# Adding the residual in layer 1 by an accumulating DMA in a two-layer graph kernel

## The chip, the cores and the metric

The kernel runs on one core of a Trainium2 chip, in float32 throughout. The metric is the device time of one execution in microseconds, as the median over several runs; lower is better. The core has TensorE (PE in the profile; PEld is its loading of weights), VectorE (DVE), ScalarE (ACT), GpSimd (POOL) and SyncE (SP). Each has its own instruction queue and works it off in order. DMAs are issued from such a queue and carried out by 16 DMA engines.

## The reference

There are 16 batches of 1024 nodes with 512 features, one dense weighted adjacency matrix of 1024 x 1024, and two residual layers.

```python
# layer 0
h = relu(layernorm(x));  x = x + (adj @ h) @ W0 + bias
# layer 1
h = relu(layernorm(x)) @ W
s1, s2 = h @ a[:F], h @ a[F:]
e   = leaky_relu(s1[:, :, None] + s2[:, None, :], 0.2) * adj
att = softmax(e, axis=2)
x   = x + elu(att @ h + beta * h)
```

The last line is the one that the change concerns. With z for the argument of elu, elu(z) = relu(z) + min(exp(z), 1) - 1. So the output is x1 + elu(z) = relu(z) + min(exp(z), 1) + (x1 - 1), where x1 is what layer 0 gave. The constant -1 is already in the bias of layer 0, so that x1 - 1 is what layer 0 writes out.

## The kernel before, in words

Layer 0 runs over the 16 batches first. For each it leaves three things in DRAM: `x1d[b]` (x1 - 1, four blocks of 128 x 1024), `ud[b]` (the normalised rows) and the logits `s1d`, `s2d`.

Layer 1 then runs over the batches, each in two stages. `layer1_a` multiplies the unnormalised attention matrix with the rows u, by a seven-product scheme in place of eight block products: 14 steps of 8 matmuls with 512 columns. `layer1_b` multiplies the outcome with W in the same way: 14 steps of 4 matmuls with 256 columns. After each step k the function `after(k)` emits the small work planned for that place: first what `later[k]` holds, then what the plan of the batch holds. All instructions keep the order in which they are emitted on their engine, and SP's DMAs too. Steps over 13 of `layer1_b` are carried over to the next batch's `layer1_a`, so that step 14 there is step 0 here.

The plan of a batch prepares the softmax of the next one. `masked` lets ScalarE form leaky_relu(s1 + s2) and VectorE multiply it by a mask row block and take the maximum; there are 8 mask blocks of 512 KB per batch, loaded by SP into the two buffers of the pool `ld`. `spread_max` sends the maxima through DRAM (`md`, `mall`) to all partitions, `exp` takes exponentials, `turn` transposes them into `pT`, `spread_sum` does with the sums what `spread_max` did (`sd`, `sall`), and `diagonal` adds beta times the sum to the diagonal. `right_sum` (`pT_T`) and `u_sums` (`ul_S`) form the operands of the seven products; `load_u` fetches the rows. In `SOFTMAX_A` (lines 1147 and following) the mask blocks 2 to 7 are asked for at the steps 0 to 5 of `layer1_a`, and the blocks 0 and 1 at the steps 11 and 12 of the preceding `layer1_b`. In batches 1 to 8 a row block of the last batch is normalised on the side (`late`).

The output of `layer1_b` comes in eight parts, each 128 x 512: node half nh, feature half oh, and q. For each part `elu` (line 884) emits:

- `parts`: ScalarE computes r = relu(z) and ez = exp(z), in two pieces each. They go to a buffer of the pool `b4` (12 buffers, also used for e and for the products) and to one of `b2`.
- `total`: two or three steps later VectorE forms d = min(ez, 1) + d, where d is a half of the tile `x1`, and GpSimd adds r to it.
- `store`: seven steps after the part, SP writes the whole tile to the output by four DMAs of 128 KB, once for two feature halves. For the four tiles these lie at steps 3, 4, 5 and 6 of the next `layer1_a`.

The tile `x1` (128 x 1024, pool `xp` with 4 buffers) is filled by `load_x1`, one SP load of 512 KB for each of four tiles at the steps 7 to 10 of `layer1_a` (line 1231). In the last batch (`end`) VectorE does both sums, and ScalarE's queue issues some of the stores.

Of the kernel before, what the change touches and what calls it, by code (L numbers as in the profile page):

```python
# [29 lines left out]
F32 = mybir.dt.float32  # L30
AF = mybir.ActivationFunctionType
ALU = mybir.AluOpType
AX = mybir.AxisListType

P = 128
Q = 32
# [29 lines left out]
def kernel(  # L66
# [12 lines left out]
    B, N, D = x.shape  # L79
# [4 lines left out]
    HD = D // 2  # L84
# [4 lines left out]
    b4 = ctx.enter_context(tc.tile_pool(name="b4", bufs=12))  # L89
    up = ctx.enter_context(tc.tile_pool(name="up", bufs=7))  # L90
    ld = ctx.enter_context(tc.tile_pool(name="ld", bufs=2))
    xp = ctx.enter_context(tc.tile_pool(name="xp", bufs=4))
# [17 lines left out]
    class InOrder:  # L110
# [9 lines left out]
    pe, dve, act, pool, sp = (  # L120
        InOrder(e) for e in (nc.tensor, nc.vector, nc.scalar, nc.gpsimd, nc.sync)
    )

    def add(o, i0, i1, op=ALU.add):
        dve.tensor_tensor(o, i0, i1, op=op)
# [368 lines left out]
    def node_rows(t, b):  # L494

        return [t[b, ts(s, SN), :].rearrange("(g q) d -> q g d", q=Q) for s in range(G)]
# [49 lines left out]
    def beside(plan):  # L546
        def run(k):
            for f, *args in plan.get(k, ()):
                f(*args)

        return run
# [49 lines left out]
    x1d = {}  # L601
# [272 lines left out]
    x1s = {}  # L874
    later = {}

    def layer1_b(b, plan):

        rs = sms[b].rs
        rows = node_rows(out, b)  # L880
        end = b == B - 1
        zs = {}

        def elu(nh, oh, q, z, k):

            r = b4.tile([P, 2, HD], F32, tag="b4", name=f"r_{b}_{nh}{oh}{q}")
            g0 = HC * nh + 2 * q
            ez = zs.pop((nh, oh, q), None)
            if ez is None:
                ez = b2.tile([P, 2, HD], F32, tag="b2", name=f"ez_{b}_{nh}{oh}{q}")  # L890

            def parts():
                for i in range(2):
                    sc = rs[:, g0 + i : g0 + i + 1]
                    act.activation(r[:, i, :], z[:, i, :], AF.Relu, scale=sc)
                    act.activation(ez[:, i, :], z[:, i, :], AF.Exp, scale=sc)

            if end or ez is not z:
                parts()
            else:  # L900
                later.setdefault(k + 1, []).append(parts)
            x1 = x1s[b, nh, q]

            def total():
                d = x1[:, :, ts(oh, HD)]
                dve.scalar_tensor_tensor(d, ez, 1.0, d, op0=ALU.min, op1=ALU.add)
                (dve if end else pool).tensor_tensor(d, d, r, op=ALU.add)

            def store():
                for s in range(G):  # L910
                    (act if end and nh and s % 2 else sp).dma_start(
                        out=rows[s][:, ts(2 * nh + q, 2), :], in_=x1[ts(s, Q)]
                    )

            later.setdefault(k + (1 if end else 2 if ez is not z else 3), []).append(total)
            if nh != oh:
                later.setdefault(k + (1 if end else 7), []).append(store)

        products = NODES_LAST if end else P5_EARLY
        at = {p[0]: 2 * n for n, p in enumerate(products)}  # L920
        weighted1 = []

        def part(nh, oh, q, ps):
            zs[nh, oh, q] = b2.tile([P, 2, HD], F32, tag="b2", name=f"z_{b}_{nh}{oh}{q}")
            act.copy(zs[nh, oh, q], ps)

        def rest(nh, oh, q, ps, k):
            z = zs[nh, oh, q]
            add(z, ps, z)
            elu(nh, oh, q, z, k)  # L930

        def done(prod, q, ps):
            if prod == "p1":
                weighted1[0].fork("W", q, ps)
            elif prod == "p6":
                part(0, 1, q, ps)
            elif prod == "p5":
                part(1, 1, q, ps)
            elif prod == "p7":
                rest(1, 1, q, ps, at[prod] + q)  # L940
            elif prod == "p3":
                rest(0, 1, q, ps, at[prod] + q)
            else:
                elu(0 if prod == "p2" else 1, 0, q, ps, at[prod] + q)

        def after(k):
            for f in later.pop(k, ()):
                f()
            beside(plan)(k)

        weighted1.append(Weighted(f"pq{b}", w1_c, done, products))
        weighted1[0].rest(0, lefts.pop(b), after)
# [66 lines left out]
    halves = [(nh, q) for nh in range(2) for q in range(2)]  # L1019
# [4 lines left out]
    for k in range(2):  # L1024
        sp.dma_start(
            out=v_bcs[k], in_=a[ts(k, D), :].rearrange("f o -> (f o)").partition_broadcast(P)
# [37 lines left out]
    def merged(*plans):  # L1064
        out = {}
        for plan in plans:
            for k, steps in plan.items():
                out.setdefault(k, []).extend(steps)
        return out
# [26 lines left out]
    def plan_out(o, b):  # L1096

        return steps(
            (-1, o.keep, 0, 1), (-1, o.keep, 1, 0), (-1, o.keep, 1, 1), (0, o.relu, 0, 0),
            (1, o.stats, 1, 0, 0), (3, o.relu, 0, 1), (4, o.stats, 1, 0, 1), (7, o.relu, 1, 0),  # L1100
            (8, o.stats, 1, 1, 0), (10, o.stats, 1, 1, 1), (13, o.relu, 1, 1),
            (2, o.logits, 0, 0, 0), (3, o.logits, 0, 0, 1), (7, o.logits, 0, 1, 0),
            (8, o.logits, 0, 1, 1), (9, o.logits, 1, 0, 0), (10, inner_left, b, "p7"),
            (12, o.logits, 1, 0, 1), (13, inner_left, b, "p3"), (15, o.logits, 1, 1, 0),
            (16, o.logits, 1, 1, 1), (16, o.store_logits), (18, inner_left, b, "p4"),
            (3, o.store, 0, 0), (6, o.store, 0, 1), (10, o.store, 1, 0), (15, o.store, 1, 1),
            (18, begin, b, "Y"), (24, begin, b, "X"),
            (8, load_res, b, 0, 0), (10, load_res, b, 0, 1), (14, load_res, b, 1, 0),
            (18, load_res, b, 1, 1),
        )  # L1110
# [16 lines left out]
    def plan_softmax(order, s):  # L1127
        names = {
            "L": [s.logits], "B": [s.blocks, 0], "b": [s.blocks, 1],
            "X": [s.spread_max, 0], "x": [s.spread_max, 1], "N": [s.top, 0], "n": [s.top, 1],  # L1130
            "S": [s.spread_sum, 0], "s": [s.spread_sum, 1],
            "D": [s.diagonal, 0], "d": [s.diagonal, 1],
        }
        for g in range(NCH):
            names[f"M{g}"] = [s.masked, g]
            names[f"E{g}"] = [s.exp, g]
            names[f"V{g}"] = [s.turn, g]
            names[f"L{g}"] = [s.load, g]
            names[f"e{g}"] = [s.load, g, b4, "b4"]
            names[f"K{g}"] = [s.keep, g]  # L1140
            names[f"R{g}"] = [s.reload, g]
        for n in ("T1", "T2", "T3", "T4"):
            for k in range(2):
                names[n + "ab"[k]] = [s.right_sum, n, k]
        return {k: [tuple(names[n]) for n in steps.split()] for k, steps in order.items()}
# [32 lines left out]
    for b in range(B):  # L1178
        plans = [plan_out(out_of, b)] if b else []
# [45 lines left out]
    for b in range(B):  # L1225
        plans = [{
            k - 14: [(f,) for f in later.pop(k)] for k in sorted(later)
        }]
        plans.append(plan_softmax(LATE_A, sms[b]))
        plans.append(steps((3, u_sums, b, 0, 1), (4, u_sums, b, 1, 1)))  # L1230
        plans.append({7 + i: [(load_x1, b, nh, q)] for i, (nh, q) in enumerate(halves)})
        plan_b = {}
        if b == 0:
            plans += [
                {12: [(w_sums, w1_c)]}, steps((-1, u_sums, b, 0, 0), (0, u_sums, b, 1, 0)),
            ]
        if b + 1 < B:
            plans.append(plan_softmax(SOFTMAX_A, sms[b + 1]))
            plans.append({k: [(load_u, b + 1, n)] for k, n in LOADS_U.items()})
            plan_b = plan_softmax(SOFTMAX_B, sms[b + 1])  # L1240
        if b + 2 < B:
            plan_b = merged(plan_b, plan_softmax(LOGITS_B, sms[b + 2]))
        if 1 <= b <= NCH:
            plan_b = merged(plan_b, {
                4: [(late.load, b - 1)], 9: [(late.stats,)], 10: [(late.relu,)],
                11: [(late.logits, b - 1)], 13: [(late.store,)],
            })
            if b == NCH:
                plan_b[13].append((late.store_logits,))
        if b + 1 < B:  # L1250
            plan_b = merged(plan_b, steps((10, u_sums, b + 1, 0, 0), (12, u_sums, b + 1, 1, 0)))
        layer1_a(b, merged(*plans))
        layer1_b(b, plan_b)
# [36 lines left out]
```

## Time and profile before

| What | Value |
|---|---|
| Median of 3 runs | 2270.57 us (2269.57 to 2272.37) |
| Profiled execution, its own time | 2272.64 us |
| Its span | 2270.9 us |
| TensorE (PE) busy | 2251.6 us, 99% |
| VectorE (DVE) busy | 1916.1 us, 84% |
| ScalarE (ACT) busy | 1540.3 us, 68% |
| GpSimd (POOL) busy | 390.2 us, 17% |
| DMA: moved, mean rate | 336.03 MB, 148 GB/s |
| Layer 1, from its first matmul to the span's end | 1098.39 to 2270.9 us |

A group line of the page reads: line, engine, operation, output <- inputs, shapes and count; then busy time and the mean of one in ns; then the idle time of the engine before them and what ended it. Every instruction carries the line of one helper (L118), so that they are told apart by their tiles: `x` is the tile x1, `e` the logits, `mask` the mask block, `xr` layer 0's rows. The windows view gives, for each stretch of time, the busy time and count of PE, PEld, DVE, ACT and POOL, then the granted clock, the share of time in which the DMA engines were busy, and GB/s. The chain of waits goes back from the last instruction: at each step to what released it, or to the instruction before it on its engine.

### The profile page before, as it was taken

The page shows a single profiled execution, that of the slowest core. Times are in us where ns is not written, and L with a number is a line of the kernel's source. Part 1 is how long each engine was busy: PE and PEld are TensorE (multiplying, and loading weights), DVE is VectorE, ACT ScalarE, POOL GpSimd, SP SyncE. Part 2 cuts the span into 40 slices and gives each one's busy share as a digit, 9 for nine tenths or more (in the row PEclk, how much of TensorE's full clock was granted, in tenths as well). Part 3 has the DMA queues.
Part 4 walks back from the last instruction along what each step waited for, and adds up shares of the span by engine and source line. Part 5 has one row for each costly group of instructions (what it writes and reads, how often), then busy time and mean ns, then how long its engine had stood idle before and what let it go on. Part 6 is the DMA issues. An engine that isn't in the chain of part 4 may idle for free.

```text
span 2270.9 us, 29732 instructions
## 1 busy us (share of the span) xinstructions
PE 2251.6 (99%) x8524; PEld 1609.2 (71%) x8524; DVE 1916.1 (84%) x4285; ACT 1540.3 (68%) x4106; POOL 390.2 (17%) x568
## 2 busy tenths in 40 slices
PE   9999999999999999999999999999999999999998
PEld 5888888888888888888566556665566556665565
DVE  7888888989898898889898888888888887888774
ACT  3766766776776767676567677767767677667753
POOL 1211111111111111110021022211222022201220
PEclk9999999999999999999999999999999999999999
DMA  6343454343444343235535554455445544455441
GB/s 212 136 134 119 148 170 142 131 147 121 130 162 164 133 147 134 101 130 205 174 113 171 185 165 149 149 187 169 152 137 169 172 158 134 130 167 169 136 129 37
DMA packets 194292, 336.03 MB, mean 148 GB/s; under 512 B 78800, under 2 KB 86992, under 8 KB 194128
## 3 DMA queue, kind: packets, MB, share of 16 engines
q1 hardware_dynamic: 193808, 333.61, 45.0%
q8 instruction: 67, 1.10, 0.2%
q14 instruction: 97, 0.79, 0.1%
q10 hardware_dynamic: 320, 0.52, 0.1%
HBM read 228.33 MB, written 109.91 MB: 149 GB/s over the span
## 4 chain that ended last, share of the span: by engine, by line
PE 82%; DVE 7%; DMA 5%; ACT 3%; SPq 2%; issue 1%; POOL 0%; DVEq 0%; ACTq 0%
PE z_Y L118 13%; PE po_Y L118 9%; PE y_Y L118 8%; PE pq_Y L118 8%; PE z_X L118 6%; PE po_X L118 5%; PE y_X L118 4%; PE pq_X L118 4%; PE z_W L118 4%; PE y_W L118 2%; PE po_W L118 2%; PE y_p3y L118 2%; PE y_p7y L118 2%; PE y_p4y L118 2%; PE y_p6y L118 2%; DMA mask<-maskd 2%
## 5 line engine op out<-in xcount | busy, mean ns | idle before, releaser
L118 POOL TENSOR_TENSOR x<-x,r 128x512 f32<-128x512 f32 x120 | 199.0, 1676 | 923.2 <-DVE x L118 366.4
L118 ACT ACTIVATE e<-e,nm 128x256 f32<-128x256 f32 x480 | 237.2, 497 | 142.0 <-DVE nm L118 142.0
L118 DVE CUSTOM_DVE_ANT_0 e<-e,mask 128x256 f32<-128x256 f32 x512 | 215.8, 478 | 108.5 <-DMA mask<-maskd 87.1
L118 PE MATMUL z_Y<-pT,ul_U 128*128 128x512 f32 x512 | 224.9, 592 | 0.0
L118 ACT ACTIVATE e<-s2b,s1b 128x256 f32<-128x256 f32 x512 | 216.4, 500 | 0.0
L118 PE MATMUL po_Y<-w_c,y_C 128*128 128x256 f32 x768 | 188.3, 379 | 0.0
L118 PEld LDWEIGHTS z_Y<-pT,ul_U 128*128 128x128 f32 x512 | 97.3, 190 | 115.6 <-issue 107.9
L118 PE MATMUL pq_Y<-w_c,z_C 128*128 128x256 f32 x768 | 174.9, 380 | 2.6 <-ACT z L118 2.6
L118 DVE CUSTOM_DVE_ANT_0 y_S<-xr,v_bc 128x512 f32<-128x512 f32 x240 | 165.3, 689 | 9.2 <-DVE s L118 0.5
L118 PEld LDWEIGHTS pq_Y<-w_c,z_C 128*128 128x128 f32 x768 | 145.3, 190 | 31.3 <-issue 7.7
L118 PEld LDWEIGHTS po_Y<-w_c,y_C 128*128 128x128 f32 x768 | 145.9, 190 | 20.3 <-ACT po_X L118 0.2
L118 DVE STREAM_TRANSPOSE pT<-e 128x512 f32<-128x512 f32 x240 | 155.7, 687 | 1.0
L118 ACT ACTIVATE h<-h,nb_h,r_h 128x512 f32<-128x512 f32 (+1 forms) x132 | 98.2, 793 | 56.9 <-POOL nb_h L118 56.9
L118 ACT ACTIVATE y_S<-xr 128x512 f32<-128x512 f32 x90 | 56.7, 630 | 91.9 <-DVE xr L118 91.4
L118 PE MATMUL po_X<-w_c,y_S 128*128 128x256 f32 x512 | 115.7, 379 | 0.0
L118 PE MATMUL pq_X<-w_c,z_S 128*128 128x256 f32 x512 | 115.6, 379 | 0.0
L118 PE MATMUL z_Y<-pT_T,ul_U 128*128 128x512 f32 x256 | 113.6, 594 | 1.8 <-DVE pT_T L118 1.6
L118 PE MATMUL z_W<-pT,ul_U 128*128 128x512 f32 x256 | 112.5, 592 | 0.0
L118 PE MATMUL z_Y<-pT_T,ul_S 128*128 128x512 f32 x256 | 112.5, 592 | 0.0
L118 PE MATMUL z_X<-pT_T,ul_S 128*128 128x512 f32 x256 | 112.5, 592 | 0.0
L118 PE MATMUL z_X<-pT,ul_S 128*128 128x512 f32 x256 | 112.5, 592 | 0.0
L118 PEld LDWEIGHTS po_X<-w_c,y_S 128*128 128x128 f32 x512 | 97.3, 190 | 13.2
(236 smaller groups left out, 5116.4 us busy)
## 6 DMA issues: line engine op xcount, KB each, us to landing
mask<-maskd SPq DMA_DIRECT2D x128, 512.0 KB
h<-in_x_dram SPq DMA_DIRECT2D x64, 512.0 KB
xr<-in_x_dram SPq DMA_DIRECT2D x256, 128.0 KB
x1d<-xr SPq DMA_DIRECT2D x64, 512.0 KB
ul_U<-ud_U SPq DMA_DIRECT2D x64, 512.0 KB
x<-x1d SPq DMA_DIRECT2D x64, 512.0 KB
out_dram<-x SPq DMA_DIRECT2D x252, 128.0 KB
ud_U<-xr SPq DMA_DIRECT2D x60, 512.0 KB
```

The source lines that it names most:

```text
L118: return lambda *args, **kwargs: tc.keep_in_program_order(f(*args, **kwargs))
```

## The change

For the batches 0 to 14, `parts` writes r straight into a half of the output tile (now named `o`, in the pool `xp`, which no load fills). `total` adds min(ez, 1) to it on VectorE as before. Once both feature halves of a tile are there, GpSimd issues one DMA of 512 KB that adds x1 - 1 from DRAM to the tile (`accum_op`), 4 per batch. The loads of x1 on SP and the sums on GpSimd are gone for these batches; the store waits for the DMA. The last batch keeps its loads and both sums on VectorE, of which the sum with r is now the first.

```diff
+        sums = {}
 
         def elu(nh, oh, q, z, k):
 
-            r = b4.tile([P, 2, HD], F32, tag="b4", name=f"r_{b}_{nh}{oh}{q}")
+            if end:
+                r = b4.tile([P, 2, HD], F32, tag="b4", name=f"r_{b}_{nh}{oh}{q}")
+            else:
+                if (nh, q) not in sums:
+                    sums[nh, q] = xp.tile([P, 2, D], F32, tag="xp", name=f"o_{b}_{nh}{q}")
+                r = sums[nh, q][:, :, ts(oh, HD)]
...
-            x1 = x1s[b, nh, q]
+            full = x1s[b, nh, q] if end else sums[nh, q]
 
             def total():
-                d = x1[:, :, ts(oh, HD)]
+                d = full[:, :, ts(oh, HD)]
+                if end:
+                    add(d, d, r)
                 dve.scalar_tensor_tensor(d, ez, 1.0, d, op0=ALU.min, op1=ALU.add)
-                (dve if end else pool).tensor_tensor(d, d, r, op=ALU.add)
+                if nh != oh and not end:
+                    pool.dma_start(
+                        out=full.rearrange("p k d -> p (k d)"), in_=x1d[b][nh, q],
+                        accum_op=ALU.add,
+                    )
 
             def store():
                 for s in range(G):
                     (act if end and nh and s % 2 else sp).dma_start(
-                        out=rows[s][:, ts(2 * nh + q, 2), :], in_=x1[ts(s, Q)]
+                        out=rows[s][:, ts(2 * nh + q, 2), :], in_=full[ts(s, Q)]
                     )
...
-        plans.append({7 + i: [(load_x1, b, nh, q)] for i, (nh, q) in enumerate(halves)})
...
+        else:
+            plans.append({7 + i: [(load_x1, b, nh, q)] for i, (nh, q) in enumerate(halves)})
```

The `else` is that of `if b + 1 < B`, so the loads remain for the last batch alone.

## The prediction

> **What bounds the kernel now.** First the page: engine shares and the costliest group.
>
> ```profile
> span 2270.9 us, 29732 instructions
> PE 2251.6 (99%) x8524; PEld 1609.2 (71%) x8524; DVE 1916.1 (84%) x4285; ACT 1540.3 (68%) x4106; POOL 390.2 (17%) x568
> ...
> L118 POOL TENSOR_TENSOR x<-x,r 128x512 f32<-128x512 f32 x120 | 199.0, 1676 | 923.2 <-DVE x L118 366.4
> ```
>
> TensorE has work almost always; half of what GpSimd does is the 120 sums that the change removes. So I cut layer 1 by batch, from one first matmul to the next (the windows view: start:end, length, busy time and count of each engine, clock, DMA share, GB/s).
>
> ```profile
> 1098.39:1170.63 72.24, 72.24 (x225) 42.56 (x225) 60.69 (x146) 47.90 (x137) 5.86 (x4) 1.00 0.51 172
> ...
> 1606.00:1679.00 73.00, 71.71 (x223) 41.84 (x222) 60.45 (x143) 50.50 (x143) 15.08 (x12) 1.00 0.51 163
> 1679.00:1752.86 73.86, 72.74 (x227) 42.69 (x226) 61.68 (x145) 51.80 (x147) 15.14 (x13) 1.00 0.50 161
> ...
> 1971.95:2044.19 72.24, 72.24 (x225) 42.56 (x225) 59.40 (x139) 51.02 (x145) 13.28 (x9) 1.00 0.47 150
> ```
>
> A batch that never waits takes 72.24 us. That is TensorE's own time, and its matmuls stay as they are. From the first batch's start to the last one's, 2188.68 - 1098.39 = 1090.29 us went by; 15 x 72.24 = 1083.60. So all that layer 1 can give before its last batch is 6.7 us (0.3%), and it lies in batches 3 to 10.
>
> Then the chain of waits inside a slow batch (start, length, what).
>
> ```profile
> 1608.34 2.95 DVE x L118 x3
> 1612.72 1.40 DVE e L118
> 1616.23 4.60 DMA mask<-maskd
> 1622.96 3.10 DMA md<-mx
> 1632.24 6.09 DMA mask<-maskd
> ...
> 1657.89 3.43 DMA sd<-sm
> 1662.65 3.34 DMA sall<-sd
> 1670.33 1.99 PE pq_Y L118 x8
> ```
>
> The next batch's softmax is a loop of VectorE work, mask loads into two buffers, and small round trips through DRAM, all issued in order by SP. Where it takes longer than 72.24 us, TensorE waits. Two more views say what swells it: the durations (min/median/max) of one VectorE sum, and the DMA share (last column but one) in two stretches of one batch.
>
> ```profile
> L118 DVE TENSOR_TENSOR ul_S<-ul_S,ul_U x32: 691/693/1649, 1102.6 to 2189.1; 128x512 f32<-128x512 f32 x32
> ```
>
> ```profile
> 1460.00:1468.00 8.00, 8.00 (x20) 3.47 (x19) 7.96 (x11) 7.93 (x21) 5.64 (x4) 1.00 0.00 0
> 1484.00:1496.00 12.00, 12.00 (x30) 5.30 (x29) 7.62 (x24) 11.86 (x42) 0.00 (x0) 1.00 0.95 309
> ```
>
> The same sum takes 0.69 us or 1.65 us. In the first stretch GpSimd is busy, VectorE is full and no byte moves; in the second the DMA engines are full and GpSimd rests.
>
> **What the Trainium skill says.** *SBUF — State Buffer*, "Who interferes with whom": a VectorE instruction with two SBUF inputs and a GpSimd instruction that reads SBUF share a port pair, and the second to come waits for the whole of the first. The 1.65 us beside 0.69 agrees. The page adds that descriptors written by GpSimd are held up by VectorE's two-port modes; a plain two-input sum, it infers, does not do so. No trace here shows it. *DMA: Bandwidth & Descriptors*, "SWDGE vs HWDGE vs iDMA" and "Issuing engines are not separate DMA queues": an accumulating DMA can only come from GpSimd, and runs on the same 16 DMA engines, which alternate between queues by packet. *Collectives: The Full Stack*, "The bandwidth ceiling": an add in the DMA engine reads two sources per write, and reduce-scatter reached 1/1.93 of all-gather. The trace has no such transfer; this ratio is my main price.
>
> **The change, part by part.**
>
> 1. GpSimd's sums go: 120 x 1.676 us, 8 in each of 15 batches. No compute engine waits for them by name, but VectorE is blocked. Excess of means over medians or over the unblocked form (VectorE's groups by form, 1098 to 2250 us): the 62 sums with ez (942 - 680 ns) 16.2 us; 480 masked products (482 - 420) 29.8; 32 ul_S from ul_S (1139 - 693) 14.3; 32 ul_S from two ul_U (917 - 681) 7.6; 16 late products (1161 - 689, layer 0's same form) 7.6. Together 75 us, or 5 us a batch, all at the head of the softmax loop, before the mask load at 1616. ScalarE is full there too (7.93 of 8 us), so some of it turns into a wait for ScalarE's e: I take 3 us a batch, bounds 1 and 5.
>
> 2. SP's 60 loads of x1 go, 4 a batch, 0.43 us of issue each (1.7 us a batch). They stand just ahead of the small transfers md and sd; in the batch from 1826 us md took 5.23 and sd 6.11 us where 3.1 and 3.43 are seen elsewhere. I take 2 us a batch off the loop, bounds 0 and 4.
>
> 3. Added: 60 accumulating DMAs of 512 KB on GpSimd, 4 a batch, each behind VectorE's second total of its tile: about 1464, 1464.5, 1466 and 1471.7 us in the batch above, some 3 us earlier without the locks. GpSimd has only the late row's four small operations of a later step behind them. A plain packet of 4096 bytes takes 159 ns in this trace, 8 rows per engine are 1.27 us, so an accumulating transfer at twice that is an estimated 2.5 us of all engines, four are 10 us. They fall into the empty 1460 to 1468. Half of the third's and the fourth's time meets the mask loads of 1469.7: those then get every other packet, 8 x (159 + 318) ns = 3.8 us instead of 1.3. The loop loses 2.5 us a batch; bounds 0 (all in the gap) and 10 us (four times a plain load, the mask loads behind all of it).
>
> 4. Each store on SP now waits for a transfer, and behind it stand the last two masks, the u loads and the second md. Stores are issued at 1481.8, 1484.3, 1486.8 and 1490.5, about 18 to 20 us after the accumulate they wait for. At 10 us of transfers and 2 us of completion this is hidden; cover ends near 5 us per transfer, four times a plain load.
>
> 5. Relu now writes into the output tile, so 8 of layer 1's allocations per batch leave the pool that e and z use, and the output tile is held from step 4 on. Its last reader is the store of step 3 to 6 one batch earlier, over 30 us before: nothing. VectorE's totals keep number, shape and place: nothing.
>
> 6. Last batch: the sum with r comes before the total. At the end r is ready one exponential (about 0.4 us) ahead of ez, and the last sum no longer follows the total: 0.4 us off the tail, bounds 0 and 0.7.
>
> Sum per slow batch: -3 - 2 + 2.5 = -2.5 us on the loop. The worst batch, 73.86 us, is 1.6 over TensorE's 72.24, so the loop would fit under TensorE and nearly all of the 6.7 us come back: I count 5.6, since the backlog differs from batch to batch, and 0.4 at the tail, 6.0 us. The profiled execution took 2272.64 us for its span of 2270.9; the median of the runs is 2270.57, 2.1 lower. So 2266.6 us for the profiled execution, and 2264.6 us for the median.
>
> **Rivals.**
>
> A, the accumulate is slow and delays masks and stores. Point of decision: the loop has 5 us (steps 1 and 2) plus what it lies under 72.24, so it turns at about three to four times a plain load's engine time. For it: nothing here shows this transfer's rate, and each of its packets holds an engine while the masks wait. Against it: the empty stretch, and 18 us of cover. At four times: -5 + 10 = 5 us on a loop already 1.2 over in the slow batches and near zero elsewhere, so 15 batches x 3 us on average = 45 us: 2315 us. This is the case that ends slower.
>
> B, VectorE's gain is swallowed by ScalarE and the mask loads, and only SP's relief counts: half of the 6.7 us returns, 2267.5 us, about no change. For it: VectorE waits for masks 87 us in all, and a faster VectorE there waits longer.
>
> C, a milder loss: descriptor writing is held up by VectorE, full at 7.96 of 8 us, so that the transfers start at 1470 instead of 1463 and meet masks and stores, at twice a plain load's price. Masks 5 us later, minus 5 from steps 1 and 2, on batches 1.2 over: 0 to +1 us in 15 batches, 2270 to 2285, say 2278.
>
> **How the numbers follow.** About 0.2% (4.5 us) is what a measurement of this kernel can tell from no change. Forecast 0.42; B and the near half of C, within it, 0.20; the rest of C 0.12; A 0.26. So faster 0.42, same 0.20, slower 0.38. Nothing beats all stalls gone plus 0.7: 2263.2, hence 2263 below. Above, A is open; 2315 leaves out about its worse half, 0.13. The forecast's own range is 2263 to 2266.
>
> **What would show it.** Right: batches of 72.2 to 72.5 us throughout, the ul_S maximum near 0.70 us, DMA share above zero in the stretch before a batch's first mask load, md near 3 us, and SP not waiting for an accumulate. Wrong: chain pieces of 7 us or more for a mask or a store held by the accumulate; packets of the new queue well over 320 ns (A); transfers that start many us after their total (C); or VectorE waiting for e and masks by what it saved (B).

## The result

The changed kernel takes 2293.96 us (median of 6 runs, 2287.82 to 2302.31), the kernel before 2271.94 us beside it (6 runs, 2269.57 to 2272.64). The ratio is 1.0102, with a 95% interval of 1.008 to 1.0123: slower by 1%, where I had forecast faster by 0.3%.

The page of the changed kernel: span and engines, the new DMA queue, and the new issues (size, median us from issue to landing).

```profile
span 2289.5 us, 29757 instructions
PE 2253.4 (98%) x8524; PEld 1609.9 (70%) x8524; DVE 1842.7 (80%) x4285; ACT 1540.5 (67%) x4106; POOL 244.0 (11%) x508
...
q0 software_dynamic: 8640, 31.46, 7.4%
...
L118 POOL DMA_DIRECT2D o<-x1d x60 | 52.7, 936 | 620.7 <-DVE o L118 558.0
...
o<-x1d POOLq DMA_DIRECT2D x60, 512.0 KB, 7.6
```

VectorE lost 73 us of busy time (1916.1 to 1842.7) and GpSimd 146 (390.2 to 244.0), with no instruction fewer on VectorE. The relief that I had looked for came. Yet the batches of layer 1, cut as before, are longer:

```profile
1170.66:1242.90 72.24, 72.24 (x226) 42.56 (x224) 55.22 (x143) 50.29 (x143) 5.65 (x8) 1.00 0.59 164
1242.90:1321.15 78.25, 74.47 (x225) 42.83 (x224) 56.95 (x145) 51.84 (x146) 5.32 (x8) 0.98 0.54 152
1321.15:1395.52 74.37, 72.50 (x225) 42.48 (x224) 56.92 (x145) 51.55 (x146) 5.32 (x8) 1.00 0.58 160
...
2060.05:2134.33 74.28, 72.51 (x225) 42.48 (x224) 54.66 (x139) 50.95 (x146) 3.48 (x4) 1.00 0.53 145
```

The first two run at TensorE's 72.24 us, the third takes 6.0 us more, and from then on each takes 73.1 to 75.3 us, also those that had no stall before. From the first batch's start to the last one's it is 1109.12 us against 1090.29. These 18.8 us are the whole loss, since the two spans differ by 18.6.

About 2 us of it came with a lower clock. In the third batch TensorE stood still for 3.8 us, and its busy time is 2.2 us longer as well (74.47): after a stop of 3.0 us it was granted half its clock for 3.4 us.

```profile
1290.36:1293.78 3.42, 3.42 (x5) 1.33 (x4) 3.35 (x6) 3.40 (x14) 0.00 (x0) 0.50 0.41 107
```

The chain of waits in the batch from 1395 us (start, length, what) answers to the one of before.

```profile
1404.32 8.79 DMA mask<-maskd
1415.11 3.08 DMA md<-mx
1421.94 5.33 DMA mask<-maskd
1431.47 3.73 DMA md<-mx
```

The first mask piece, which is the load of block 3 from its request to its landing, took 4.6 us and takes 8.8. Over all batches, VectorE's own waits name the same thing (us in total, times, longest), first in the changed kernel, then before:

```profile
DVE e L118 <- DMA mask<-maskd: 161.8, 50, 6.1
```

```profile
DVE e L118 <- DMA mask<-maskd: 87.1, 41, 4.7
```

So there are 74.7 us more of waiting for masks, 5.0 per batch, in the place of 73.4 us less work. Why the masks are late is to be seen in the first 16 us of a batch (windows view; DMA share is the last column but one) and in GpSimd's and SP's timelines of that batch, which starts at 1321.15. The line in the second box is the later of the two stretches in the kernel before, in the batch that starts at 1460.02.

```profile
1321.15:1329.15 8.00, 8.00 (x20) 3.61 (x19) 5.82 (x19) 7.93 (x21) 2.65 (x3) 1.00 0.54 88
1329.15:1337.15 8.00, 8.00 (x20) 3.54 (x19) 2.83 (x13) 6.66 (x16) 0.86 (x1) 1.00 1.03 265
```

```profile
1468.02:1476.02 8.00, 8.00 (x20) 3.61 (x19) 6.05 (x28) 6.64 (x16) 1.94 (x2) 1.00 0.48 151
```

```profile
1323.56 0.90 POOL L118 DMA_DIRECT2D o<-x1d  x1 [5.33 <-DVE o L118]
1325.32 1.74 POOL L118 DMA_DIRECT2D o<-x1d  x2 [0.86 <-DVE o L118]
1331.03 0.86 POOL L118 DMA_DIRECT2D o<-x1d  x1 [3.96 <-ACT e L118]
```

```profile
1328.35 11.85 SPq L118 DMA_DIRECT2D mask<-maskd  x4
```

The transfers are issued at 2.4, 4.2, 4.8 and 9.9 us into the batch. SP asks for mask block 2 at 7.2 us, when VectorE has freed its buffer, and for block 3 at 8.8. In the second stretch the DMA engines are full and VectorE, at 2.83 of 8 us, waits.

The queues (packets, MB, share of the 16 engines) tell who has the engines: first in the 2.8 us from the request for block 2 on, then in the next 3 us. q0 carries the accumulates, q1 the loads that SP asks for. The last line is the kernel before, in the 2.8 us from its request on (1469.69).

```profile
q0 software_dynamic: 151, 0.54, 101.9%
```

```profile
q0 software_dynamic: 123, 0.47, 78.7%
q1 hardware_dynamic: 68, 0.28, 24.4%
```

```profile
q1 hardware_dynamic: 147, 0.54, 61.7%
```

At first the masks get no packet at all. The first one starts 3.6 us after the request, where before it started after 1.0. The packets of the first three accumulates run from 4.0 to 13.5 us into the batch, those of the fourth, which is issued after both requests, from 14.4 to 18.6, beside block 3.

### The profile page after: what moved, and what is told of

The parts are those of the page before. It is cut to its first block, busy times and chain, and to the rows that moved or that the text cites. A ratio compares the mean times of both kernels' runs of the same rounds, so it can differ in the third digit from the quotient of the medians.

```text
span 2289.5 us, 29757 instructions
## 1 busy us (share of the span) xinstructions
PE 2253.4 (98%) x8524; PEld 1609.9 (70%) x8524; DVE 1842.7 (80%) x4285; ACT 1540.5 (67%) x4106; POOL 244.0 (11%) x508
## 4 chain that ended last, share of the span: by engine, by line
PE 70%; DMA 12%; DVE 8%; ACT 5%; SPq 3%; issue 2%; POOL 1%; DVEq 0%; ACTq 0%; POOLq 0%
PE po_Y L118 9%; PE pq_Y L118 8%; PE y_Y L118 8%; PE z_Y L118 8%; DMA mask<-maskd 7%; PE po_X L118 5%; PE y_X L118 5%; PE pq_X L118 4%; DVE e L118 3%; DMA md<-mx 3%; SPq L118 3%; PE y_W L118 2%; PE pq_W L118 2%; PE y_p7y L118 2%; PE y_p3y L118 2%; PE po_W L118 2%
## 5 line engine op out<-in xcount | busy, mean ns | idle before, releaser
L118 DVE CUSTOM_DVE_ANT_0 e<-e,mask 128x256 f32<-128x256 f32 x512 | 190.8, 421 | 189.2 <-DMA mask<-maskd 161.8
L118 POOL DMA_DIRECT2D o<-x1d x60 | 52.7, 936 | 620.7 <-DVE o L118 558.0
L118 PEld LDWEIGHTS z_Y<-pT_T,ul_U 128*128 128x128 f32 x256 | 48.0, 192 | 87.3 <-issue 52.7
```

What stands on the lines that cost most here:

```text
L118: return lambda *args, **kwargs: tc.keep_in_program_order(f(*args, **kwargs))
```

## The experiments

Theory 1: the accumulating DMAs occupy the 16 DMA engines, about 10.5 us per batch (4 transfers, 8 packets of 328 ns on each engine), just when the mask blocks 2 and 3 are asked for; the softmax loop grows beyond TensorE's 72.24 us. Its rivals: the stores that wait for the landing hold SP (2), the rest of the change costs it (3), something of the accumulate itself, such as its long packets or its read of the tile, rather than its total time (4), and every transfer costs its share wherever it lies (5). All ratios below are to the kernel before, run beside them on the same chip.

**e1: a plain DMA in the same place.** Tile, issue and waits stay.

```diff
                     pool.dma_start(
                         out=full.rearrange("p k d -> p (k d)"), in_=x1d[b][nh, q],
-                        accum_op=ALU.add,
                     )
```

> The changed kernel, but GpSimd's 60 DMAs overwrite the tile instead of adding to it (relu and min(exp, 1) are lost from the output of the batches 0 to 14): same place, same waits, one read fewer per write. Theory 1 (the loss is engine time of the DMAs just ahead of the mask loads: 328 ns per packet of 4096 bytes, 10.5 us per batch): packets fall to about 160 ns, 5 us per batch, the mask pieces of 8 to 10 us fall to 5 to 6, and the time to about 2270 to 2278 us. Rival 2 (it is the issue from GpSimd and the place, or the stores' wait for the landing, whatever the DMA does): 2288 us or more.

2266.38 us, ratio 0.9981 (0.9974 to 0.9988). Packets of 4096 bytes on the new queue took 159 ns at the median, where the accumulate's took 328. From first to last batch it is 1084.82 us, 1.2 over TensorE's own 1083.60. This is below what I expected, since I had reckoned with a rest of the loss. Issue from GpSimd, the place and the waits cost next to nothing; what the accumulate adds to a plain DMA there costs 28 us.

**e2: no DMA at all.**

```diff
                 dve.scalar_tensor_tensor(d, ez, 1.0, d, op0=ALU.min, op1=ALU.add)
-                if nh != oh and not end:
-                    pool.dma_start(
-                        out=full.rearrange("p k d -> p (k d)"), in_=x1d[b][nh, q],
-                        accum_op=ALU.add,
-                    )
```

> The changed kernel without GpSimd's 60 DMAs (x1 - 1 is left out of the output of the batches 0 to 14). Theory 1: with no DMA ahead of the masks only the relief of VectorE and SP is left, every batch near 72.24 us, 2263 to 2267 us. Rival 3 (the loss comes from the rest of the change, such as r kept in the output tile and other buffers in the pools): 2280 us or more.

2265.45 us, ratio 0.9979 (0.9971 to 0.9987); all 15 batches take 72.24 us, 1083.60 in sum. Rival 3 falls. The relief of VectorE and SP is worth the whole 6.7 us that layer 1 had to give in the profile, if nothing is put in their way.

**e3: the kernel before without GpSimd's sums.**

```diff
-                (dve if end else pool).tensor_tensor(d, d, r, op=ALU.add)
+                if end:
+                    add(d, d, r)
```

> The kernel before without GpSimd's 120 sums (r is left out of the output of the batches 0 to 14); the loads of x1 stay on SP. It prices the port conflict alone. If VectorE's 5 us per batch reach the loop: 2264 to 2267 us. If ScalarE and the mask loads swallow them: 2269 to 2272 us, as before.

2266.22 us, ratio 0.998 (0.9973 to 0.9988), 1083.60 us from first to last batch. GpSimd's sums alone held all of the 6.7 us; without them VectorE's busy time is 1849.5 us, and the loads of x1 on SP don't hurt.

**e4: the changed kernel, with mask block 2 asked for early.** The plan letters are: `L` a mask load into the two buffers of `ld`, `e` one into `b4`, `M` the masked product.

```diff
-        0: "M0 L2 M1 L3", 1: "M2 L4", 2: "M3 L5 X", 3: "M4 L6", 4: "M5 L7", 5: "N B E0",
+        0: "M0 L3 M1 L4", 1: "M2", 2: "M3 L5 X", 3: "M4 L6", 4: "M5 L7", 5: "N B E0",
...
-    LOGITS_B = {8: "L", 11: "L0", 12: "L1"}
+    LOGITS_B = {8: "L", 11: "L0", 12: "L1 e2"}
```

> The changed kernel complete, but mask block 2 goes into a buffer of the larger pool and is asked for together with block 1, some 8 us ahead of the accumulating DMAs, and the blocks 3 to 5 one buffer turn earlier than before. Theory 1: the first wait behind the DMAs goes, the loop gets 5 us of slack, 2266 to 2280 us. Rival 2 (the stores that wait for the landing hold SP and what is behind them): the landing is where it was, so 2288 us or more.

2266.29 us, ratio 0.998 (0.9972 to 0.9987), 1083.98 us from first to last batch, with the output complete. Its timelines in one batch:

```profile
1448.68 1.37 SPq L118 DMA_DIRECT2D mask<-maskd  x3
```

```profile
1463.06 0.91 POOL L118 DMA_DIRECT2D o<-x1d  x1 [5.33 <-DVE o L118]
1464.83 1.75 POOL L118 DMA_DIRECT2D o<-x1d  x2 [0.86 <-DVE o L118]
1470.53 0.86 POOL L118 DMA_DIRECT2D o<-x1d  x1 [3.96 <-DVE mx L118]
```

The three first masks are asked for 14 us ahead of the first accumulate. The accumulates are issued and land as in the changed kernel (median 7.6 us), and the stores wait for them as there. Rival 2 falls: what hurt was the mask behind the accumulates that VectorE needs first.

**e5: twice a plain DMA.** e1, and behind each DMA a second one of the same size, to a spare tensor in DRAM.

```diff
                     pool.dma_start(
                         out=full.rearrange("p k d -> p (k d)"), in_=x1d[b][nh, q],
                     )
+                    pool.dma_start(out=spare[nh, q], in_=x1d[b][nh, q])
```

> The plain DMA of e1 in the place of the accumulate, and behind it a second plain one of the same 512 KB from DRAM to a spare place in DRAM (elu is lost from the output of the batches 0 to 14). Engine time as with the accumulate, nothing read from the tile. Theory 1 (engine time just ahead of the mask loads, whatever kind): the masks late as with the accumulate, 2285 to 2300 us. Rival 4 (something of the accumulate itself, its packets of 328 ns holding an engine or its read of the tile): near e1, 2266 to 2272 us.

2310.47 us, ratio 1.0187 (1.0168 to 1.0207). The shares of the new queue, of e1 and of e5, show the doubled time.

```profile
q0 software_dynamic: 8640, 31.46, 4.0%
```

```profile
q0 software_dynamic: 10560, 62.92, 7.2%
```

7.2% of e5's span of 2300.2 us is 166 us, and 7.4% of the changed kernel's 2289.5 is 169: the same engine time without any accumulate gives a loss of the same kind, and a larger one (most of the first mask pieces in its chain take 9 to 10 us). So neither the add nor the read of the tile is needed for it. Rival 4's other half, packets that hold an engine long, isn't settled by this run: its second DMAs move packets of 32768 bytes, 1213 ns each at the median. e6 and e10 below bear on it, since their packets are those of the accumulate.

**e6 and e9: two of the four accumulates per batch**, the two issued first or the two issued last.

```diff
-                if nh != oh and not end:
+                if nh != oh and not end and not nh:
```

> The changed kernel with the accumulate for the two tiles of node half 0 only, which are issued first (x1 - 1 is left out of the other half of the output of the batches 0 to 14). 5.2 us of engine time per batch in place of 10.5, done before mask block 2 is asked for. Theory 1 (only what still runs when the masks are asked for counts): 2264 to 2268 us. Rival 5 (every accumulate costs its share): half the loss over e2, about 2280 us.

> The changed kernel with the accumulate for the two tiles of node half 1 only, which are issued last (x1 - 1 is left out of half 0 of the output of the batches 0 to 14): the same bytes as in e6, beside the requests for mask blocks 2 and 3. If the place decides: the mask waits grow over those of e6 and the time lies over it, about 2272 to 2285 us. If the amount decides: e6's 2267 us.

e6, with `not nh`: 2267.14 us, ratio 0.9987 (0.998 to 0.9993). e9, with `nh`: 2266.87 us, 0.9982 (0.9973 to 0.9991). e6 did as theory 1 said, although its packets are as long as the changed kernel's: long packets alone don't cost the time. e9 did not: its transfers still run when the masks are asked for, and yet it loses nothing. VectorE's waits for masks (105.9 us in e6, 117.7 in e9) did grow with the later place, but the loop still fits. So at this amount the place inside these few microseconds doesn't decide.

**e10: three accumulates per batch.** The line of e6 with `not (nh and q)`.

> The changed kernel with three of the four accumulates per batch (x1 - 1 is left out of the last quarter of the output rows' groups of the batches 0 to 14), 7.9 us of engine time. With e6 (two, no loss) and the changed kernel (four, 25 us over two) it says where the loss begins. Theory 1 (a threshold: nothing until the loop is longer than TensorE's 72.24 us, then batch by batch): between 2266 and 2278 us, below the middle of the two. Rival 5 (in proportion): about 2280 us.

2276.66 us, ratio 1.0026 (1.002 to 1.0033), 1092.06 us from first to last batch. With 5.2 us of engine time per batch next to nothing is lost, with 7.9 about 9.5 us in all (over e6), with 10.5 about 27. Had each transfer cost its share (rival 5), e6 would have lost half of what the changed kernel loses. It is a threshold, as theory 1 has it, and with the last-issued transfers left out it lies between two and three. e10's own time says less: it is inside theory 1's range, but only 3 us under rival 5's 2280.

One number sorts all twelve profiled kernels: when VectorE begins on mask block 3 (its first masked product, median of the batches 1 to 14). Where that is at 11.5 to 14.3 us into the batch (e1 to e4 and e6 to e9), layer 1 lies at most 1.2 us over TensorE's 1083.60. In the kernel before it is at 15.3 us (6.7 us over), in e10 at 15.7 (8.5), in the changed kernel at 17.3 (25.5) and in e5 at 18.2 (35.7). This also says why e5 loses more than the changed kernel: its block 3 comes later still.

**e7 and e8: the early mask for the kernel before, and two early masks for the changed one.** e7 is e4's edit made to the kernel before. e8 takes block 3 along (`"L1 e2 e3"`, and `"M0 L4 M1 L5"`, `"M2"`, `"M3 X"` in the steps after).

> The kernel before, complete, with the same early load of mask block 2 as e4. If the early mask alone makes e4 fast, this is near 2266 us too and the accumulate gives nothing; if e4 needs GpSimd's sums gone, the port conflict stays and this is 2268 to 2271 us.

> The changed kernel, complete, with the mask blocks 2 and 3 both asked for ahead of the accumulating DMAs. Theory 1: block 3's wait goes as well, but TensorE's pace is already reached with block 2 alone, so 2263 to 2267 us, equal to e4.

e7: 2266.87 us, ratio 0.9983 (0.9977 to 0.999). e8: 2265.99 us, 0.9976 (0.9969 to 0.9983), with 1083.60 us from first to last batch. Both beat both kernels. e7 gets there with the loads and the sums of before, so beside the same early mask (e4, 0.998 beside e7's 0.9983) the accumulating DMA gives nothing that these runs can tell from nothing.

## Why the prediction was wrong, point by point

**The bound.** That layer 1 can give 6.7 us at most, because TensorE needs 72.24 us per batch, was right: e2 and e8 reach 1083.60 us and stop there. The 2.1 us that I took off for the median were too many: with the stalls gone, e2's median lies only 0.9 us under its profiled run.

**Step 1, the port conflict.** Right in kind and size. The sum that took 0.69 or 1.65 us now has one duration (min/median/max):

```profile
L118 DVE TENSOR_TENSOR ul_S<-ul_S,ul_U x32: 691/692/693, 1102.8 to 2207.0; 128x512 f32<-128x512 f32 x32
```

Of 75 us that I counted, 73.4 left VectorE's busy time. In the loop it brought the request for mask block 2 forward by 2.6 us (from 9.8 to 7.2 us into the batch at the median), where I took 3.

**Step 2, SP's loads.** SP's waits for sd in layer 1 fell from 126.6 to 58.0 us and those for md from 99.8 to 85.9. It is in the right direction; e3 shows that it wasn't needed.

**Step 3, the accumulating DMAs, is the step that failed.** The price of a packet was right: an estimated 318 ns, measured 328. The sum built on it was not. I let one mask load pass by the tail of the transfers, 3.8 us in place of 1.3, and put 2.5 us on the loop. Three things were wrong in it.

First, the times. The working moved the transfers 3 us forward, to 1.0, 1.5, 3.0 and 8.7 us into the batch, but left the masks' request at 9.7, although its own step 1 moves that too. Measured, the transfers are issued at 2.4, 4.2, 4.8 and 9.9 us, since ScalarE's z and VectorE's totals come only then, and the blocks 2 and 3 are asked for at 7.2 and 8.8. So both requests fall while the first three transfers run.

Second, the sharing. A mask load was to get every other packet from its request on. It got no packet for 3.6 us, against 1.0 before, so the alternation that step 3 built on isn't what the trace shows there. Why not is open.

Third, the count. Block 3 queues behind block 2 and then meets the fourth transfer; without that one (e10) 17 of the 27 us are gone. The chain's piece for block 3 is 8.8 us instead of 4.6, in other batches 7.6 to 10.4. That is 4.2 us in place of my 2.5, against the 2.6 us that step 1 really gave, so that VectorE begins on block 3 about 2 us later than before. The DMA engines had been empty there because VectorE was late, and with VectorE early the masks moved into the same hole.

**The margin.** The sum of -2.5 us should have left a loop under 72.24 us. It had a cover of 5 us in steps 1 and 2 on paper, and on this I placed the turn at three to four times a plain load's engine time for four transfers. e6 and e10 show it between 5.2 and 7.9 us per batch, so below twice a plain load's time for all four, and e1 shows one plain load's time (5.1 us) to be nearly free. That the loss begins only in the third batch fits a lead of the softmax over TensorE that the first two batches used up; no run measured this lead by itself.

**Step 4, stores.** Right. Landing took 5.2 to 11.6 us against a cover of 18, and SP waited for an accumulate once, for 23.5 us, at the turn to the last batch where no mask stands behind it.

**Step 5, buffers.** Right: e2 keeps that part and reaches TensorE's pace. **Step 6, the tail.** From the last batch's start to the end of the span it was 82.35 us and is 82.00: 0.35 us, where I had 0.4. Six of the eight other runs with this last batch lie at 81.6 to 82.0 us too, but e6 and e9 at 82.46 and 82.34, so that it is likely and not shown.

**The rivals.** A had the mechanism (masks behind the transfers) and the direction, but asked for four times a plain load's time; twice was enough. Its stores never mattered. C had the size of the masks' delay, with a wrong cause: GpSimd began 0.3 to 0.6 us after the total, and its 0.87 us of descriptor writing (at most 1.19) shows no such delay beside a busy VectorE. Its sum came out near zero because it too set the full 5 us of steps 1 and 2 against the delay. B is refuted by e3: with the accumulates out of the way, ScalarE and the masks didn't swallow VectorE's gain.

## What to carry to other kernels

An empty stretch of the DMA engines is not free room if the wait that keeps it empty is the one the change removes: place the new transfers and the old requests on the same, shifted clock before adding them up. When a transfer doubles its engine time, as this accumulate did, count every load that is asked for while it runs, with those queued behind, and not the first alone; and don't take for granted that a load shares the engines from its request on. And a loop with little slack answers by a threshold: ask for its first input earlier, into a buffer that is free at that time, before adding anything beside it; here this alone gave the whole gain.

## What the runs showed of the hardware that was not expected

- An accumulating DMA moved packets of 4096 bytes in 328 ns and a plain one in 159 ns, from the same queue and in the same place: a ratio of 2.06, with hardly any spread (327 to 336 ns from the tenth to the ninetieth percentile).
- GpSimd needed 866 ns (median) to write the descriptors of one accumulating DMA of 512 KB, and 530 ns for the plain one.
- Landing after issue took 7.6 us for the accumulate and 4.9 us for the plain DMA beside the same traffic.
- While accumulates filled the engines, a mask load's first packet came 3.6 to 4.0 us after its request, and 0.95 us after it in the kernel before.
- The changed kernel's runs spread over 14.5 us (2287.82 to 2302.31), those of before over 3.1 us. The granted clock, as a mean over the span, was 0.997 to 0.998 in the three shortest of the changed kernel's runs and 0.994 to 0.996 in the three longest. Only one of these runs has a trace; there, the one stretch at half clock in layer 1 followed a stop of TensorE of 3.0 us.
